# A conditioned mixture-of-experts layer on one core: input buffers, routing pace, split order and due times rearranged

## The chip, the core and the metric

The kernel runs on one core of a Trainium2 chip. The metric is the device time of one execution in microseconds. The engines are named as in the profile: PE is TensorE (PEld its weight loads), DVE is VectorE, ACT is ScalarE, POOL is GpSimd, and SP is SyncE, which here only issues transfers.

## The reference, cut to what matters

8 x 1024 tokens with 512 channels pass through a modulated linear layer, then through a shared gated unit and a routed mixture of 64 experts, 8 of them for each token. The result is added to the input.

```
y  = clip(((x * styles) @ weight.T) * dcoefs + bias, -256, 256)     # styles, dcoefs from cond_512
shared = silu(y @ sh_gate_w) * (y @ sh_up_w) @ sh_down_w            # 512 -> 1024 -> 512
topk_idx, w = route(sigmoid(y @ router_w.T), e_bias)                # 8 groups, best 4, then 8 of 64 experts
for each expert e and its tokens:                                   # 512 -> 256 -> 512
    o = silu(y @ gate_w[e]) * (y @ up_w[e]) @ down_w[e]
    routed[token] += w * o
out = x + shared + routed
```

## The kernel before, in words

All matrix products run in a rounded 32-bit format. Each operand is split into a high part (an ACT copy) and a low part (a DVE subtraction, `split`, L75 its ACT copy, and `sub`, L72), and three products hi·hi, hi·lo, lo·hi are summed in PSUM. So each raw tile that arrives costs one ACT and one DVE instruction before PE can read it.

The work has three stages.

*Conditioning* (to about 240 us). For each of 16 token tiles of 512 tokens (`NT`, `TT`), the modulated layer gives y. It goes to DRAM twice: row by row (`y_d`, for the experts' gathers) and transposed in four slices of 128 channels (`yT_d`, for the shared unit). The last tile, 15, stays in SBUF.

*Shared unit and routing* (240 to 1316 us). `order` is tile 15 first, then 0 to 14; each has `HC` = 8 steps of 128 hidden channels, 128 steps in all, `i` counting them. A step has `gate_up` (24 matmuls, L124), the hidden product in `hidden` (ACT silu, DVE product, split), and `down` of the step before (12 matmuls, L1081). PSUM holds the four sums of a tile in `acc`; at the first step of the next tile `finish` adds the residual rows to them (L1104, DVE) and sends them out (L1105, SP). In the first tile, each step also fetches and splits the shared weights of later steps: `fetch_dn` (L807, tile dnr) and `fetch_gu` (L144, tile gur). In the last steps of each tile `fetch_y` (L1064, tile yr) fetches the four slices of the next tile's y, which `load_y` splits into yh and yl a step later, and `fetch_res` (L1099, tile xn) fetches four blocks of residual rows in the last one. dnr, gur and yr share one tag, "gur", with two buffers; xn has four of its own. All four kinds are issued by SP, in program order; SP waits at an issue until the buffer's last reader is done.

Between these, `route_slots` is a generator that computes on DVE, for eight chunks of 1024 tokens, which slot of which expert each token takes. After each step the loop draws from it as much as a credit allows (`credit`, L1180); each yield gives a cost. What it has ready is scattered by POOL, five per step (`write`, L1051), into a table that the last steps read.

In the last steps the first expert units are begun by hand (`early`, `early_x`): step 126 and step 127 each turn two blocks of gathered rows by PE (L541, into the one pt buffer), split them (xh at L544, xl), and split half of the first unit's gate and up weights (gh at L552, gl).

*Experts* (from 1316 us). 156 units of up to four blocks of 128 slots (20 of one, 16 of two, 120 of four; the last four units, 152 to 155, have 4, 1, 4, 4). A unit gathers its rows (POOL, L537), transposes and splits them, multiplies by gate and up in four parts of 12 matmuls (L564, L573 for the one-block units), takes the hidden product, and for each block does a down of 6 matmuls (L584), weighs it on ACT (oc, L588) and adds it to the output by an indirect transfer of POOL (`scatter`, L591). As two units can hold the same token, the scatters of a unit wait until all those of the unit before it have landed (`chain`). A unit's down needs the whole hidden product's low part; its hidden product's split and its down weights' split wait for the downs of the unit two before it, whose buffers they take. The order of all this is made ahead of time: `plan` gives each task an engine, a length, a lag and a due time; `arrange` simulates the engines and always takes, of the tasks ready on an engine, the one that is due first. The due time of a down is the unit's `ddue` plus the pair from `DOWN`:

```
DOWN = {1: (-8.2, 1.0), 2: (6.6, 5.1), 4: (6.6, 5.1)}
ddue + DOWN[u.nb][0] + DOWN[u.nb][1] * s
```

For a unit of four blocks, `ddue` is 13.76 after the unit's own due time, and the next unit is due 17.76 after it (its 4 x 2.73 of gate and up and 4 x 1.71 of turns and downs).

## Time and profile before

| what | value |
|---|---|
| median of three runs | 3730.5 us (3728.97 to 3731.85) |
| the profiled execution | 3734.11 us |
| its span, first to last instruction | 3732.3 us |
| mean granted TensorE clock | 0.996 |
| first and last matmul | 4.95 us, 3708.1 us |

PE is busy nearly all the span; matmuls overlap in the records, so a busy PE does not by itself say how closely they follow each other, and the distance from start to start is read from the timeline. Engine names with a q (SPq) are issues of transfers, which do not count as busy. The views that the prediction uses are the list of who waited for whom, the timeline of one engine in a window, and the table of windows, whose columns are the stretch and its length, the busy time and instructions of PE, PEld, DVE, ACT and POOL, the granted clock of PE, the DMA engines' busy share and their GB/s.

### The profile page before, as it was taken

Reading aid. Unit: us, or ns where it says so; the run is one execution under the profiler, and the core shown is the slowest. Engines: PE = TensorE matmul, PEld = TensorE weight load, DVE = VectorE, ACT = ScalarE, POOL = GpSimd, SP = SyncE. Lnnn points to the kernel's source line nnn. Section 1 sums busy time; section 2 is a strip of 40 time slices with the busy share of each in tenths; the row PEclk is TensorE's granted clock in tenths of the full one; section 3 lists DMA queues with packets and bytes.
Section 4 is the critical chain, followed back from the end, with each engine's and each line's share of the span. In section 5 each row is a group of like instructions: output and inputs, shape, how many; then the busy total and the mean of one; then the engine's idle time right before and its main releaser. Section 6 shows DMA issues by size and latency. Waiting matters only on the chain. (4 is left out here: it accounts for less than half of the span.)

```text
span 3732.3 us, 49590 instructions
## 1 busy us (share of the span) xinstructions
PE 3686.6 (99%) x17819; PEld 3051.5 (82%) x17819; DVE 2006.0 (54%) x3196; ACT 1736.3 (47%) x2676; POOL 2090.1 (56%) x1597
## 2 busy tenths in 40 slices
PE   8999999999999999999999999999999999999997
PEld 7777888888888888888888888888888888888886
DVE  6766666666552255555455554555555555555553
ACT  6652112111111155555555565555555555555554
POOL 0003676666654055666676666666656656666653
PEclk9999999999999999999999999999999999999998
DMA  8862212222122267777777777777777777777664
GB/s 256 239 173 64 66 35 52 52 47 57 37 50 60 99 166 157 152 150 158 147 141 153 161 183 166 177 177 192 143 174 147 168 145 175 166 157 130 117 118 58
DMA packets 238739, 491.23 MB, mean 132 GB/s; under 512 B 43074, under 2 KB 75858, under 8 KB 230803
## 3 DMA queue, kind: packets, MB, share of 16 engines
q0 software_dynamic: 135840, 280.28, 40.3%
q1 hardware_dynamic: 101651, 206.63, 18.0%
q8 instruction: 142, 2.33, 0.3%
q10 hardware_dynamic: 992, 1.06, 0.1%
q14 instruction: 114, 0.93, 0.1%
HBM read 443.20 MB, written 195.63 MB: 171 GB/s over the span
## 5 line engine op out<-in xcount | busy, mean ns | idle before, releaser
L591 POOL DMA_INDIRECT out<-oc,tokw x532 | 915.6, 1721 | 662.4 <-ACT oc L588 197.8
L564 PE MATMUL pg<-xh,gh 128*128 128x512 f32 (+1 forms) x2176 | 838.7, 385 | 0.0
L1051 POOL DMA_INDIRECT tab_d<-tokw,ad x512 | 566.2, 1106 | 485.3 <-DVE h L136 203.7
L564 PE MATMUL pg<-xh,gl 128*128 128x512 f32 (+1 forms) x2176 | 823.5, 378 | 0.0
L564 PE MATMUL pg<-xl,gh 128*128 128x512 f32 (+1 forms) x2176 | 821.6, 378 | 0.0
L537 POOL DMA_INDIRECT xg<-y_d,tokw x532 | 594.6, 1118 | 357.6 <-PE pt L541 138.5
L72 DVE TENSOR_TENSOR xl<-pt,xh 128x512 fp32r<-128x512 f32 x532 | 352.6, 687 | 413.6 <-ACT xh L544 360.9
L588 ACT ACTIVATE oc<-po,tokw 128x512 f32<-128x512 f32 x532 | 367.6, 691 | 318.0 <-PE po L584 263.2
L564 PEld LDWEIGHTS pg<-xh,gl 128*128 128x128 f32 x2176 | 409.1, 188 | 78.6
L564 PEld LDWEIGHTS pg<-xl,gh 128*128 128x128 f32 x2176 | 409.6, 188 | 71.7
L564 PEld LDWEIGHTS pg<-xh,gh 128*128 128x128 f32 x2176 | 408.8, 188 | 71.1
L584 PE MATMUL po<-dh,hh 128*128 128x512 f32 x1064 | 427.9, 402 | 0.0
L711 DVE TENSOR_TENSOR hf<-hf,pg 128x512 f32<-128x512 f32 x240 | 164.9, 687 | 483.8 <-PE pg L564 458.6
L584 PE MATMUL po<-dh,hl 128*128 128x512 f32 x1064 | 418.1, 393 | 0.0
L584 PE MATMUL po<-dl,hh 128*128 128x512 f32 x1064 | 415.3, 390 | 0.0
L124 PE MATMUL gu<-yh,guh 128*128 128x512 f32 x1024 | 400.9, 391 | 3.4 <-ACT yh L75 3.4
L72 DVE TENSOR_TENSOR gl<-wg,gh 128x1024 fp32r<-128x1024 f32 x312 | 376.2, 1222 | 51.3 <-ACT gh L552 49.3
L124 PE MATMUL gu<-yl,guh 128*128 128x512 f32 x1024 | 401.3, 392 | 0.2 <-DVE yl L72 0.2
L124 PE MATMUL gu<-yh,gul 128*128 128x512 f32 x1024 | 398.8, 389 | 0.0
L544 ACT CAST xh<-pt 128x512 fp32r<-128x512 f32 x532 | 296.9, 587 | 192.4 <-PE pt L541 134.3
L552 ACT CAST gh<-wg 128x1024 fp32r<-128x1024 f32 x312 | 324.1, 1049 | 27.0 <-PE pg L564 23.4
L708 ACT ACTIVATE hf<-pg 128x512 f32<-128x512 f32 x240 | 144.0, 600 | 293.0 <-PE pg L564 279.3
(246 smaller groups left out, 5203.3 us busy)
## 6 DMA issues: line engine op xcount, KB each, us to landing
wg<-in_wexp SPq DMA_DIRECT2D x156, 1024.0 KB
wd<-in_wexp SPq DMA_DIRECT2D x156, 512.0 KB
y_d<-yt SPq DMA_DIRECT2D x64, 256.0 KB
xn<-in_x SPq DMA_DIRECT2D x64, 256.0 KB
out<-xn SPq DMA_DIRECT2D x64, 256.0 KB
xr<-in_xT SPq DMA_DIRECT2D x60, 256.0 KB
yT_d<-yf SPq DMA_DIRECT2D x60, 256.0 KB
yr<-yT_d SPq DMA_DIRECT2D x60, 256.0 KB
```

What stands on the lines that cost most here:

```text
L72: V.tensor_tensor(o, a, b, ALU.subtract)
L124: i_ = PE.matmul(p_, lhsT=w_[:, q * KC + k], rhs=y_[k], start=n == 0, stop=n == 3 * KC - 1)
L537: queued(GP.indirect_dma_start(xg[g % RXG].bitcast(F32), None, y_d, IOA(slot_tok[:, u.block + s:u.block + s + 1], 0)))
L544: S.copy(xh[u.xq][:, :, s * P:(s + 1) * P], pt_of(g).bitcast(F32))
L552: S.copy(a[u.q][:, sl], (wg, wg, wd)[c][u.kind][:, sl])
L564: PE.matmul(out, lhsT=w_[u.q][:, c:c + P], rhs=x_[u.xq][:, k, :w], start=n == 0, stop=n == 3 * KC - 1)
L584: PE.matmul(po[d % 2], lhsT=h_[u.q][:, k, s * P:(s + 1) * P], rhs=w_[u.q][:, k * C:(k + 1) * C], start=n == 0, stop=n == 5)
L588: S.mul(oc[d % ROC], po[d % 2], slot_w[:, u.block + s:u.block + s + 1])
L591: i_ = queued(GP.indirect_dma_start(out, IOA(slot_tok[:, u.block + s:u.block + s + 1], 0), oc[d % ROC], None, compute_op=ALU.add))
L708: si = add((i, "si", m), "ACT", 0.61, 0.15, due + 5.46 * m + 3.1, lambda b=b, f=f: S.activation(hf[f % 3], pg[b % 4], AF.Silu), p, *wait_h ...
L711: mu = add((i, "mu", m), "DVE", 0.69, 0.15, t0, lambda b=b, f=f: V.tensor_tensor(hf[f % 3], hf[f % 3], pg[(b + 1) % 4], ALU.mult), si, p)
L1051: i_ = GP.indirect_dma_start(places, IOA(ad, 0), tw, None)
```

## The change: four edits

1. The slices of the next tile's y (`fetch_y`) are allocated under the tag "xn" with four buffers, together with the residual rows, in place of the tag "gur".
2. The credit of routing is 2.7 for steps 1 to 4, 1.4 for steps 5 to 8 and 2.7 after that; it was 3.4 for steps 1 to 7 and 2.7 after that.
3. In the last two steps, the first two gathered blocks' turn and split come ahead of the weights' split.
4. For the last four units, the due times of the downs are `ddue` + 2.0 + 3.0 s, whatever the number of blocks.

```diff
-                add((i, "down", s), "PE", 1.37, 0.5, ddue + DOWN[u.nb][0] + DOWN[u.nb][1] * s, lambda ...
+            first, step_ = (2.0, 3.0) if len(units) - n <= 4 else DOWN[u.nb]
...
+                add((i, "down", s), "PE", 1.37, 0.5, ddue + first + step_ * s, lambda ...
...
         def fetch_y(j, k):
-            gur["y", j, k] = xb.tile([P, TT], F32, name="yr", tag="gur")
+            gur["y", j, k] = xb.tile([P, TT], F32, name="yr", tag="xn", bufs=4)
...
-                xn[s] = xb.tile([P, C], F32, name="xn", bufs=4)
+                xn[s] = xb.tile([P, C], F32, name="xn", tag="xn", bufs=4)
...
                 if last >= 0:
+                    early_x(2 * last)
                     early(0, "wh", last)
                     early(0, "wl", last)
-                    early_x(2 * last)
...
-                credit = min(credit, 0.0) + (0.0 if not i else 3.4 if i < HC else 2.7)
+                credit = min(credit, 0.0) + (0.0 if not i else 2.7 if i < 5 or i > HC else 1.4)
```

More of the change, by code (lines that the diff above doesn't have):

```diff
@@ L724, in plan @@
                 nd += 1
-                add((i, "down", s), "PE", 1.37, 0.5, ddue + DOWN[u.nb][0] + DOWN[u.nb][1] * s, lambda u=u, s=s, d=d: down_c(u, s, d), *lo, T[i, "wl", 2], get(dns.get(d - 2)))
+                add((i, "down", s), "PE", 1.37, 0.5, ddue + first + step_ * s, lambda u=u, s=s, d=d: down_c(u, s, d), *lo, T[i, "wl", 2], get(dns.get(d - 2)))
                 dns[d] = (i, "oc", s)
```

## The prediction

> **What bounds the kernel now.** I read the page first, then the waits of PE, then the timelines around each wait, last the chain that ended last. The page and the list of PE's waits:

> ```profile
> span 3732.3 us, 49590 instructions
> PE 3686.6 (99%) x17819; PEld 3051.5 (82%) x17819; DVE 2006.0 (54%) x3196; ACT 1736.3 (47%) x2676; POOL 2090.1 (56%) x1597
> ...
> PE py L319 <- DVE xl L303: 6.1, 8, 1.4
> PE ps L260 <- DMA cd<-in_condT: 4.9, 1, 4.9
> PE gu L124 <- ACT yh L75: 3.4, 2, 2.9
> PE py L319 <- ACT xh L302: 3.3, 3, 1.5
> PE pt L541 <- DVE xl L72: 2.4, 2, 1.2
> PE po L1081 <- ACT dnh L75: 0.7, 1, 0.7
> PE po L1081 <- DVE dnl L72: 0.5, 2, 0.2
> ```

> TensorE is busy in 3686.6 of 3732.3 us. Its matmuls of 512 columns start 0.227 us apart (timeline of PE, 322.08 to 322.31), so the span is TensorE's work plus a few holes. No instruction of that work is removed. An edit can pay only in a hole, and the holes sum to 45.7 us: 4.9 before the first matmul, some 16.6 in the waits above, 24.2 after the last matmul (it ends at 3708.1), where this page does not count TensorE at all. The waits of L319 and L260 (14.3 us together) lie in the conditioning stage, which the change does not touch. Left are three places: gu/dnl around 307 to 322 us, pt at 1305 and 1315, and the end.

> **Place 1: the first shared tile, 307 to 322 us.** Timelines of SP, ACT, DVE and PE (start, length, engine, line, operation; in brackets the idle time before it and what ended that):

> ```profile
> 307.55 0.33 SPq L807 DMA_DIRECT2D dnr<-in_shdn  x1
> 308.16 3.74 SPq L1064 DMA_DIRECT2D yr<-yT_d  x2
> ...
> 315.88 0.62 ACT L75 CAST yh<-yr 128x512 fp32r<-128x512 f32 x1 [3.79 <-DMA yr<-yT_d]
> ...
> 316.55 0.80 PE L124 MATMUL gu<-yh,guh 128*128 128x512 f32 x1 [2.94 <-ACT yh L75]
> ...
> 316.50:322.50 6.00, 5.95 (x15) 4.47 (x16) 5.07 (x10) 1.72 (x4) 0.00 (x0) 0.58 0.14 52
> ```

> The fourth slice of the next tile's activations (the second yr issue in the SP row, at 311.57) waited on SP for a buffer of tag gur: the DVE row of dnl ends at 311.54. It lands after 4.3 us (315.88), and L124 sits idle. All four slices share two gur buffers with the raw weights, so each waits for an older split. Behind the idle the granted clock falls: 0.58 of full in the last row's stretch, matmuls 0.427 us apart instead of 0.235. Excess over 0.235 us, start to start: 0.41 at 307.58 (dnl, held up by 5.2 us of routing on DVE from 299.76 to 304.95), then 0.58, 0.49, 0.11, 3.10, 0.49, 0.36 from 312.15 to 317.88, then nine at 0.19. Sum 0.41 + 5.13 + 1.73 = 7.3 us.

> After the change, yr draws on the four xn buffers, empty in this tile. SP does the same eight issues, but the slices stand behind nothing older than gur's turn for their step: slice 0 right behind the issue at 286.82, slice 1 behind the dnr that becomes free at 294.5 (dnl split), slices 2 and 3 behind the one that becomes free at 295.9 (gul split). Issues take 0.33 us, landing 4.3: the last is there by 301.5, while gate_up of the new tile starts at 309.8. Next suspect is DVE: with 2.7 of routing per step for four steps and 1.4 for steps 5 to 8 instead of 3.4, one column pass of 2.5 us (1.13 + 0.69 + 0.69) stands where two stood at 299.76; hl and dnl of that step move up by 2.6 us, and the last yl ends near 307.7. Both causes go. **Gain 7.3 us**; if a slice is still late by one split pair (0.62 + 0.69) and its clock is kept, some 6.

> What this costs: routing counts its steps in the generator's credit. Its first chunk now ends at step 10 instead of 7 (20.6 units of cost at the smaller allowances), so the slot writes begin three steps of 8.2 us later, last one near 1178 + 25 = 1203 us. They go at five per step (8.2 us) and are never read before 1233 us (step 119, holding). 30 us of cover; nothing on TensorE.

> The residual rows now wait on SP for the splits of the same buffers. At the tile turn of 456 us they were issued at 440.88; the last yl there ends at 446.46, so the last row block is issued 4 us later than before and lands near 451. The add that uses it comes at 456.17, behind the last down; the next tile's first down, which needs the PSUM banks, at 462.6. Cover 5 us to the adds and some 9 to TensorE. Cost nothing. In turn, yr waits for the out transfer of the rows (issued to 459.0, landing some 4 us), against a first use two steps before the next turn: over 25 us of cover. Behind a blocked SP stand only transfers of the same kinds, in the same order.

> **Place 2: seam to the experts.** Timeline of DVE and PE:

> ```profile
> 1303.40 1.23 DVE L72 TENSOR_TENSOR gl<-wg,gh 128x1024 fp32r<-128x1024 f32 x1 [0.26 <-ACT gh L552]
> 1304.54 0.68 DVE L72 TENSOR_TENSOR xl<-pt,xh 128x512 fp32r<-128x512 f32 x1
> ...
> 1305.28 0.53 PE L541 MATMUL pt<-idr,xg 128*128 128x128 f32 x4 [1.21 <-DVE xl L72]
> ```

> There is one pt buffer, so the second transpose waits for xl of the first, and xl stands behind gl (1.23) in DVE's order, as xh behind gh (1.05) in ACT's. With the x split ahead, xh can start where gh did (1302.3), xl where hl ends (1303.14, at most 0.1 more), and ends at 1303.85, before the down ends (1304.07 by its issue). Start-to-start excess at the two places: 1.36 and 1.34. **Gain 2.7 us**; lower end 2.2 if semaphores take 0.25 each. The weight split becomes 1.3 us later: it ends near 1314.3 in the last step, and unit 0's first matmul is due at 1316.3 by then. Two us of cover; without it, 1.3 us back.

> **Place 3: the end.** Timeline of POOL (the last scatter-adds; 3704.16 is unit 154's fourth, the four below it unit 155's):

> ```profile
> 3687.32 1.56 POOL L591 DMA_INDIRECT out<-oc,tokw  x1 [7.04 <-ACT oc L588]
> 3692.95 1.56 POOL L591 DMA_INDIRECT out<-oc,tokw  x1 [4.07 <-DMA out<-oc,tokw]
> 3698.44 1.56 POOL L591 DMA_INDIRECT out<-oc,tokw  x1 [3.94 <-ACT oc L588]
> ...
> 3704.16 1.56 POOL L591 DMA_INDIRECT out<-oc,tokw  x1 [0.30 <-issue]
> 3712.12 1.58 POOL L591 DMA_INDIRECT out<-oc,tokw  x1 [6.40 <-ACTq L1193]
> ...
> 3717.75 1.56 POOL L591 DMA_INDIRECT out<-oc,tokw  x1 [0.30 <-issue]
> ```

> A unit's scatters wait until the unit before has landed: 3.9 to 6.4 us after the last instruction's end. The chain of waits ends in the same four rows. By the planner's rule (lowest due of the ready tasks), count from the last unit's due time: its four gate/up parts are due at 0, 2.73, 5.46, 8.19; unit 154's downs at 2.6, 7.7, 12.8, 17.9 before (13.76 + 6.6 + 5.1 s - 17.76), at -2, 1, 4, 7 after. So all four go ahead of the last part; in the trace two of them came behind it (3699.77). Unit 152's downs likewise move up, so its fourth scatter leaves near 3678 instead of 3687.32 and 153's follows near 3684 to 3686. Unit 154's four then leave as their downs allow: about 3694, 3696, 3699.6 and 3701.5.

> The price: two downs (12 x 0.227 = 2.7 us) leave the place where they hid the last unit's silu product and split (3699.77 to 3702.11: 2.34 us). Part 4 now ends at 3702.5, hl at 3704.8, the first down starts at 3704.9: **a new TensorE hole of 2.4 us** right at the end. First oc ends 2.26 later as before (3699.77 to 3702.03), POOL follows 0.27 later: 3707.4; four at a pitch of 1.87 start the last at 3713.0 instead of 3717.75: 4.7 us. The 13.0 us behind it (3719.31 to 3732.3) stay. From this go 0 to 2 us if unit 154's last landing (3703 + 3.9 to 6.4) is late for 3707.4, and 0 to 1.2 for the clock. For the clock: the fall at 314.7 came when TensorE had stood 1.1 us in one piece and 1.75 in the 3.4 us before; pieces of 1.41 and 1.34 at 85.8 and 87.6 left it at full. A hole of 2.4 falls above these more often than not, and would slow six of the first down's matmuls by 0.19 each. **Gain 4.2 us**, range 1.5 to 4.7. It can't turn to a loss: POOL was 8.9 us behind the first oc it could have taken.

> [...]

> **Sum.** 7.3 + 2.7 + 4.2 = 14.2 us. The profiled execution took 3734.1 us (span 3732.3 and 1.8 around it), so it would take 3719.9. The median of the three runs is 3730.5, 3.6 below; taking the gain off it gives **3716.3 us**.

> **Rivals.**
> - *Only the first tile and the seam pay.* If unit 154's last landing still sets the last four scatters (landing after a group of four took 6.4), or the planner's order is not what the chip can follow, the end gives 0 to 1.5: 3719 to 3720.5. For it: that landing was the longest; against: 154's scatters are now spread over 7.5 us. 15%.
> - *The yr wait is the transfer's, not the buffer's.* If landing stays late because the conditioning stage's writes of yT_d are slow, place 1 keeps its 7 us: 3723.3, hardly over the bound of 0.2%. Against: the issue itself stood still until 311.57, and the DMA share is 0.15 at 300 to 307 us. 6%.
> - *Slower: the residual rows starve the tile turn.* Sharing xn puts the row fetch behind the yl splits. It decides once a row block lands more than some 13.5 us after issue (446.5 against 460): from there every us is paid at 14 tile turns. At 2 us over it is 28 us: 3744. For it: SP is in order and one late split blocks all behind it. Against: 4.3 us landing, DMA share 0.3. 4%.
> - *The change doesn't do what it says*: the order of instructions at the seam or in the tail is the same. Each part is in program order or in the due times, so I give it 2%, at 3728.

> The forecast keeps 73%. Its own range is 3715 to 3719; with the first rival and the spread of the three runs (2.9 us) the range is 3713.5 to 3721.5. A measurement here tells about 0.2% (7.5 us) from no change. Faster than that: forecast, first rival, and half of the second, with some of the unnamed lost: 0.89. Within 0.2%: 0.06. Slower: 0.05.

> **What would show it.** L124's wait for yh and L1081's for dnl are gone, the granted clock stays at 1.0 at 300 to 325 us, and the four yr issues stand before 297. PE's wait for xl at L541 is gone. The first POOL issue of the last four comes about 4 us after unit 154's landing, and PE shows a new wait of about 2.4 us for hl ahead of the last four downs. It would be wrong if DVE or SP showed a new wait at the tile turns (L1104 behind in_x), or unit 0's first matmul waited for gl.

## The result, and the profile after

The changed kernel takes 3717.19 us in the median of seven runs (3715.85 to 3720.26), beside 3730.5 (3728.7 to 3732.13) of the kernel before: 13.3 us less, ratio 0.9965 with a 95% interval of 0.9955 to 0.9975. 3716.3 was forecast. On another chip it took 3718.24 beside 3731.68, ratio 0.9963 [0.9950, 0.9977].

The page and PE's waits of the changed kernel (lines of the shared stage stand two further down: L1081 is now L1083, L1064 L1066, L1099 L1101):

```profile
span 3716.6 us, 49611 instructions
PE 3684.8 (99%) x17819; PEld 3053.1 (82%) x17819; DVE 2005.9 (54%) x3196; ACT 1736.5 (47%) x2676; POOL 2086.7 (56%) x1597
...
PE py L319 <- DVE xl L303: 4.3, 4, 1.4
PE py L319 <- ACT xh L302: 2.7, 3, 1.2
PE po L584 <- ACT hh L713: 0.8, 1, 0.8
```

The waits of L124 for yh and yl and of L541 for xl are gone, L1083 keeps only its first one at 256 us, and a new one has come: L584 for hh. The same matmuls run in a span 15.7 us shorter. To see where, I split the span at four marks that both traces have.

| from, to | before | after | change | forecast |
|---|---|---|---|---|
| start, first shared down | 256.80 | 256.13 | -0.7 | 0 |
| to the eighth shared down (tile 15's last) | 65.74 | 58.36 | -7.4 | -7.3 |
| to the first expert matmul | 996.30 | 993.43 | -2.9 | -2.7 |
| to the end of the last scatter | 2400.47 | 2394.87 | -5.6 | -4.2 |
| to the end of the span | 13.02 | 13.79 | +0.8 | 0 |

The first and last rows are scatter between executions: in the nine profiles of kernels with this conditioning stage the first shared down starts between 255.9 and 257.9 us, and in all eleven profiles 12.5 to 14.2 us lie behind the last scatter. The three rows between sum to 15.9; the medians show 13.3, with 9.3 to 16.8 in the interval. The kernel before has one profile, whose execution took 3.6 us more than its median, and that of the changed kernel took 1.2 more than its own. So the distances show where the time went in one execution of each. How much of the 15.9 us other executions gain is not shown; the 1.7 us of slow matmuls in the first tile, for one, stand in that single profile of before.

### The profile page after: what moved, and what is told of

The parts are those of the page before. It is cut to its first block, busy times and chain, and to the rows that moved or that the text cites. A ratio compares the mean times of both kernels' runs of the same rounds, so it can differ in the third digit from the quotient of the medians.

```text
span 3716.6 us, 49611 instructions
## 1 busy us (share of the span) xinstructions
PE 3684.8 (99%) x17819; PEld 3053.1 (82%) x17819; DVE 2005.9 (54%) x3196; ACT 1736.5 (47%) x2676; POOL 2086.7 (56%) x1597
## 4 chain that ended last, share of the span: by engine, by line
PE 98%; DVE 1%; DMA 0%; ACT 0%; issue 0%; POOL 0%; SPq 0%; ACTq 0%; DVEq 0%; POOLq 0%
PE pg L564 38%; PE po L584 20%; PE gu L124 19%; PE po L1083 9%; PE pt L541 4%; PE py L319 4%; PE pg L573 1%; PE plt L344 1%; DMA xr<-in_xT 0%; PE psm L367 0%; ACT yf L325 0%; DVE yl L72 0%; PE pg L578 0%; DVE yt L356 0%; PE ps L1004 0%
## 5 line engine op out<-in xcount | busy, mean ns | idle before, releaser
L591 POOL DMA_INDIRECT out<-oc,tokw x532 | 915.9, 1722 | 663.4 <-ACT oc L588 203.5
L72 DVE TENSOR_TENSOR xl<-pt,xh 128x512 fp32r<-128x512 f32 x532 | 352.6, 687 | 406.6 <-ACT xh L544 405.7
L588 ACT ACTIVATE oc<-po,tokw 128x512 f32<-128x512 f32 x532 | 367.6, 691 | 316.4 <-PE po L584 279.6
L584 PE MATMUL po<-dh,hh 128*128 128x512 f32 x1064 | 428.1, 402 | 0.8 <-ACT hh L713 0.8
L584 PE MATMUL po<-dh,hl 128*128 128x512 f32 x1064 | 418.2, 393 | 0.0
L584 PE MATMUL po<-dl,hh 128*128 128x512 f32 x1064 | 415.3, 390 | 0.0
L72 DVE TENSOR_TENSOR gl<-wg,gh 128x1024 fp32r<-128x1024 f32 x312 | 376.2, 1222 | 52.0 <-ACT gh L552 51.4
L124 PE MATMUL gu<-yl,guh 128*128 128x512 f32 x1024 | 400.2, 391 | 0.0
L124 PE MATMUL gu<-yh,guh 128*128 128x512 f32 x1024 | 399.7, 390 | 0.0
L124 PE MATMUL gu<-yh,gul 128*128 128x512 f32 x1024 | 398.1, 389 | 0.0
L552 ACT CAST gh<-wg 128x1024 fp32r<-128x1024 f32 x312 | 323.9, 1048 | 27.1 <-PE pg L564 27.1
```

The lines of the kernel that those rows point to most:

```text
L72: V.tensor_tensor(o, a, b, ALU.subtract)
L124: i_ = PE.matmul(p_, lhsT=w_[:, q * KC + k], rhs=y_[k], start=n == 0, stop=n == 3 * KC - 1)
L552: S.copy(a[u.q][:, sl], (wg, wg, wd)[c][u.kind][:, sl])
L584: PE.matmul(po[d % 2], lhsT=h_[u.q][:, k, s * P:(s + 1) * P], rhs=w_[u.q][:, k * C:(k + 1) * C], start=n == 0, stop=n == 5)
L588: S.mul(oc[d % ROC], po[d % 2], slot_w[:, u.block + s:u.block + s + 1])
L591: i_ = queued(GP.indirect_dma_start(out, IOA(slot_tok[:, u.block + s:u.block + s + 1], 0), oc[d % ROC], None, compute_op=ALU.add))
```

## The experiments

**One edit taken back at a time.** Four kernels on one chip, each the changed one with one edit as before, called e1 to e4; the four hunks are those of the four kernels in the order of the expectations.

```diff
-            gur["y", j, k] = xb.tile([P, TT], F32, name="yr", tag="xn", bufs=4)
+            gur["y", j, k] = xb.tile([P, TT], F32, name="yr", tag="gur")
...
-                credit = min(credit, 0.0) + (0.0 if not i else 2.7 if i < 5 or i > HC else 1.4)
+                credit = min(credit, 0.0) + (0.0 if not i else 3.4 if i < HC else 2.7)
...
-                    early_x(2 * last)
                     early(0, "wh", last)
                     early(0, "wl", last)
+                    early_x(2 * last)
...
-            first, step_ = (2.0, 3.0) if len(units) - n <= 4 else DOWN[u.nb]
+            first, step_ = DOWN[u.nb]
```

> The changed kernel with the four y slices back in the two gur buffers; routing, split order and due times as changed. Theory (the buffers were the wait): the fourth slice is again issued only behind the split of the last shared down weights. With less routing those splits come some 2.5 us earlier than in the kernel before, so the slice is issued near 308 to 309 us and lands near 313; gate_up of the second tile (L124) waits 2 to 4 us for yh, the clock may fall behind it, and the down that follows starts at 317 to 320 us instead of 314.5. Median 3720 to 3723. Rival (routing on VectorE was the wait): that down stays at 314.5 and the median at 3717.

> The changed kernel with the routing credit of before (3.4 for steps 1 to 7), the y slices in xn. Theory (the buffers): the slices are issued before 297 us all the same; what is left is the 0.4 us wait for dnl near 307 and at most 1 us for a late yl, so the down behind the second tile's first gate_up starts at 315 to 316 us; median 3717 to 3719. Rival (routing was the wait): a wait for yh or yl of 3 us or more is back near 312 to 316 us, median 3721 or more.

> The changed kernel with the weights' split ahead of the gathered rows' split again. Theory: two waits of pt for xl of 1.2 us each are back, and from there PE is 2.7 us later to the end; median 3719.5 to 3720.5. Rival (the seam is hidden by later slack, since the experts' stage has buffers to spare): the two waits are back but the last matmul is not later; median 3717.

> The changed kernel with the due times of before for the last four units. Theory: no wait of PE at the end, the last matmul 1.2 to 1.4 us earlier against the start of the last unit's parts, but the last unit's scatters wait 6.4 us for the landing of the unit before and the last one starts 9.6 us behind the last matmul instead of 2.7; span 4.9 us longer, median 3721.5 to 3722.5. Rival (the end was bound by the matmuls, so the hole eats the gain): span the same within 1 us.

| kernel | first to eighth shared down | to first expert matmul | to end of last scatter | last matmul's end behind the first expert matmul | median us |
|---|---|---|---|---|---|
| before (median on this chip) | 65.74 | 996.30 | 2400.47 | 2389.25 | 3731.0 |
| changed (from the result above) | 58.36 | 993.43 | 2394.87 | 2390.63 | 3717.19 |
| e1: y slices in gur | 59.60 | 993.46 | 2394.86 | 2390.57 | 3720.89 |
| e2: old credit | 58.36 | 993.42 | 2394.83 | 2390.63 | 3718.17 |
| e3: weights first | 58.34 | 996.33 | 2394.97 | 2390.64 | 3720.96 |
| e4: old due times | 58.36 | 993.38 | 2400.54 | 2389.26 | 3721.47 |

(Ratios to before with their intervals, in the order of the last four: 0.9972 [0.9961, 0.9982], 0.9963 [0.9949, 0.9977], 0.9973 [0.9963, 0.9984], 0.9974 [0.9962, 0.9985]. They overlap; the distances do not.)

Each edit shows in its own distance and in no other: routing, with the buffers changed, in none (e2). The split order is worth 2.9 us and the due times 5.7, each in one profiled execution. The medians agree with these sizes only in part: e1, e3 and e4 lie 2.7, 2.8 and 3.3 us above e2, where the distances put 1.2, 2.9 and 5.7 (the median of e3 is 0.5 us above its expected range). So the profiles tell where an edit acts; its size over many executions is sure to a few us only. At the end the two theories of e4 part clearly: with the old due times TensorE finishes 1.4 us sooner, and the last scatter 5.7 us later. The scatters bound the end.

In the first tile the answer is not the one that I had laid down for e1. Either edit by itself does nearly all: the buffers alone give the whole 7.4 (e2), and less routing alone 6.1 (e1). The down behind the second tile's first gate_up starts at 315.53 us, where I had expected 317 to 320. The median of e1 lay in its range all the same; of the 3.7 us above the changed kernel its profile explains 1.2, so that hit was luck. SP and PE of the kernel with the slices in gur:

```profile
302.99 3.75 SPq L1066 DMA_DIRECT2D yr<-yT_d  x2
...
311.47 0.51 PE L124 MATMUL gu<-yh,guh 128*128 128x512 f32 x1 [0.50 <-ACT yh L75]
312.20 0.50 PE L124 MATMUL gu<-yl,guh 128*128 128x512 f32 x1 [0.22 <-DVE yl L72]
```

The fourth slice (second of the x2, 306.41) does wait for a gur buffer again, but it leaves 5.2 us earlier than before (311.57), or 4.3 counted from the first shared down, where I had expected 2.5. In the trace of before, DVE had a routing pass too many at two places of the same chain of buffers: ahead of the dnl behind which the first slice leaves (289.33 to 291.92), and ahead of the hl and the dnl behind which the third leaves (302.37 to 304.96). Counted in the same way, the first slice leaves 1.0 us earlier in e1 and the third 4.3. A third pass too many, ahead of the last dnl (308.05 to 310.63), cost nothing: that dnl waited for its high part on ACT. What is left of the wait, 0.7 us idle, did not bring the clock down (1.00 from 300 to 316 us; from 312.54 on the matmuls start 0.23 us apart), so the 1.7 us of slow matmuls go with it. The wait was thus no single cause: late splits and scarce buffers in series, and it is enough to break one.

**The size of the new hole (e5).** The last unit's downs take the second half of the hidden product first.

```diff
-        for k in range(2):
+        for k in (1, 0) if u.i == 155 else (0, 1):
```

> The changed kernel, but the last unit's downs multiply the second half of the hidden product (k = 1) before the first. Theory (the new hole was 1.4 us and not 2.4 because the three k = 0 matmuls of the first down need only the first half's split, which is done long before): now the first matmul has to wait for the second half's low part or high part, the three matmuls no longer fill the hole, so PE's wait for ACT or DVE grows from 0.8 to 1.5 to 2.2 us, the last matmul ends 0.5 to 0.9 us later against the start of the last unit's first part and the last scatter starts 0.5 to 0.9 us later; the clock may fall if most of the hole lies in one stretch of 3.4 us. Rival (the hole is set by ACT's or PSUM's order, not by which half is needed): the hole stays at 1.4 us.

PE in the changed kernel, and then in this one:

```profile
3691.33 0.39 PE L564 MATMUL pg<-xh,gl 128*128 128x512 f32 x1
3691.56 0.39 PE L584 MATMUL po<-dh,hh 128*128 128x512 f32 x1
3691.78 0.39 PE L584 MATMUL po<-dl,hh 128*128 128x512 f32 x1
3692.01 0.39 PE L584 MATMUL po<-dh,hl 128*128 128x512 f32 x1
3693.22 0.50 PE L584 MATMUL po<-dh,hh 128*128 128x512 f32 x1 [0.82 <-ACT hh L713]
```

```profile
3693.07 0.39 PE L564 MATMUL pg<-xh,gl 128*128 128x512 f32 x1
3694.95 0.50 PE L584 MATMUL po<-dh,hh 128*128 128x512 f32 x1 [1.50 <-ACT hh L713]
```

In the changed kernel three matmuls of the first down run straight behind the last part, since they read the first half, split by 3685.73. With the halves exchanged the idle time grows from 0.82 to 1.50 us, by those three matmuls (3 x 0.227). Excess of the starts over 0.235 us, all of it: 1.34 us against 2.01. The last matmul ends 0.6 us later and the last scatter 0.5 (2395.36 behind the first expert matmul). This kernel has a single run, 3720.29 us, so the reading rests on the distances. The theory holds.

**How long the chain at the end is (e6).** The earlier due times for the last two units alone.

```diff
-            first, step_ = (2.0, 3.0) if len(units) - n <= 4 else DOWN[u.nb]
+            first, step_ = (2.0, 3.0) if len(units) - n <= 2 else DOWN[u.nb]
```

> The changed kernel with the earlier due times for the last two units alone (units 154 and 155). Theory (the end is a chain of scatters through units 152, 153, 154 and 155, each waiting for the landing of the one before, and unit 154's split also waits for unit 152's last down): unit 152's last down stays late, and nearly all of the 5.6 us at the end is lost: last scatter's start 4 to 6.5 us later against the experts' first matmul than in the changed kernel, median about 3721 to 3722. Rival (only the unit next to the last matters): the last scatter as in the changed kernel, median 3717.

POOL's scatters at the end, first of the changed kernel (unit 152's fourth, 153's, the first and fourth of 154's, 155's first), then the same of this one:

```profile
3666.57 2.51 POOL L591 DMA_INDIRECT out<-oc,tokw  x1 [0.30 <-ACT dh L552]
3673.36 1.56 POOL L591 DMA_INDIRECT out<-oc,tokw  x1 [4.28 <-ACT xh L544]
3680.48 1.56 POOL L591 DMA_INDIRECT out<-oc,tokw  x1 [5.55 <-ACT oc L588]
...
3690.00 1.56 POOL L591 DMA_INDIRECT out<-oc,tokw  x1 [2.52 <-ACT oc L588]
3695.60 1.58 POOL L591 DMA_INDIRECT out<-oc,tokw  x1 [4.04 <-ACT oc L588]
```

```profile
3677.54 1.56 POOL L591 DMA_INDIRECT out<-oc,tokw  x1 [7.04 <-ACT oc L588]
3683.06 1.56 POOL L591 DMA_INDIRECT out<-oc,tokw  x1 [3.96 <-DMA out<-oc,tokw]
3688.74 1.56 POOL L591 DMA_INDIRECT out<-oc,tokw  x1 [4.11 <-ACT hf L708]
...
3694.33 1.56 POOL L591 DMA_INDIRECT out<-oc,tokw  x1 [0.30 <-ACT hh L713]
3700.93 1.58 POOL L591 DMA_INDIRECT out<-oc,tokw  x1 [5.04 <-ACT oc L588]
```

With two units, 152's fourth scatter leaves at 3677.54 and holds up the three units behind it, one landing each; 154's four come in one burst, whose landing takes 5.0 us instead of 4.0. The last scatter starts 2397.44 us behind the first expert matmul, against 2393.31 with four units and 2398.97 with none: 1.5 of the 5.7 us are gained. Median 3721.64, ratio 0.9973 [0.9962, 0.9983]. The chain theory holds, at the lower end of its 4 to 6.5 us.

**What is left: the conditioning stage (e7 to e9).** In all these kernels L319 still waits 7 to 9 us for xl and xh near 70, 87 and 133 us. There the table of slots is cleared by five transfers of 832 KB. This version clears in ten of half the size.

```diff
-                if 3 <= j < 8:
+                if 3 <= j < 13:
                     clear(j - 3)
-                if j == 9:
+                if j == 13:
...
-                if j == 11:
+                if j == 14:
                     constants()
...
-    ...f=4)[:, 2 * r:2 * r + 2], ... to_broadcast([E * NR // 40, 2, 8 * P])
+    ...f=4)[:, r:r + 1],         ... to_broadcast([E * NR // 40, 1, 8 * P])
```

> The changed kernel, with the clearing of the slot table in the conditioning stage in ten transfers of half the size over tiles 3 to 12 instead of five over tiles 3 to 7; the two steps on the token numbers that must come behind it move from tiles 9 and 11 to 13 and 14. Theory (the waits of L319 for xl and xh at 69 to 138 us stand behind the clearing transfers in the DMA engines, whose share is 0.86 to 0.90 there): L319's waits, 7.0 us in the changed kernel, fall to 2 to 4 us, one or both falls of the clock (1.7 us each) go, and the first shared down starts 3 to 7 us earlier than 256 us; median 3711 to 3715. Rival (the share is 0.84 to 0.91 at 160 to 220 us too, so the same waits come back later in the stage): the first shared down at 255 to 257 us, median 3717.

> The changed kernel as it stands, beside the one with the spread clearing, on the same chip. Theory (its own first execution was typical): the first shared down at 256 to 258 us, three waits groups of L319 near 70, 87 and 133 us with one to three falls of the clock, the last scatter starting 2393 to 2394 us behind the experts' first matmul; median 3716 to 3719, ratio to before 0.996 to 0.997. Rival (the profiled execution flattered the change): the sum of the three distances is more than 2 us longer than the 15.8 us less than before that its first profile shows.

> The kernel with the spread clearing, once more, beside the changed kernel on the same chip. Theory (the clearing held up the x slices and cost falls of the clock): the first shared down 2.5 to 4.5 us before that of the changed kernel in the same call, one fall of the clock in the conditioning stage instead of two or three, median 2 to 4 us below it. Rival (its first execution was a lucky phase of the clock's windows): first shared down and median within 1.5 us of the changed kernel's.

The kernel with the spread clearing took 3714.68 us the first time (e7), ratio to before 0.9955 [0.9941, 0.9968]. The second time (e9) it took 3715.54 (3712.81 to 3715.92) with the same ratio, beside 3718.24 (3716.85 to 3718.65) of the changed kernel on that chip (e8). The first shared down starts at 253.33 and 253.31 us; the changed kernel's second profile has it at 256.13, like its first. One fall of the clock is left in the stage (at 131.1 or 86.7 us) where the changed kernel has three in its first profile (22.1, 86.9, 134.7) and two in its second (23.5, 132.7). L319's waits, 7.0 and 8.9 us in the changed kernel's two profiles, are 6.0 and 5.8, where I had expected 2 to 4 to be left, and the start of the shared stage moves by 2.8 us, where I had expected 3 to 7. So the clearing as it was is at most a part of the cause. The edit also moves the two steps on the token numbers, which no run separates from it, and waits and falls do not add up to the 2.8 us in either pair; which transfer held up which slice is not shown. Still, the kernel beats both others, by 2.7 us in the medians of the same chip, and no run of the one lies in the range of the other. The second run of the changed kernel repeats the three distances (58.36, 993.41, 2394.87), so its first profile was typical.

## Why the prediction was right, and where a size was off

*Bound and sum.* That an edit could pay only in TensorE's holes or behind its last matmul held: 15.9 us by the profiles' three distances and 13.3 by the medians, 14.2 forecast. The median of 3717.19, 0.9 us from the forecast, is closer than the spread of its own runs and than the terms below, so part of that closeness is luck. The first two rivals, none of the gain at the end or 7 us still lost in the first tile, did not come about. Nor did the tile turns starve: TensorE has no wait there, and at the turn of 448 us the row blocks are issued by 438.2, the adds start at 448.1, so the cover was about what the text said.

*First tile.* The size was right (7.3 forecast, 7.4 between the two profiles), and the clock holds 1.00 from 300 to 325 us where it was 0.86. The slices are issued at 287.48, 293.30, 294.70 and 295.42, before 297 as forecast; SP of the changed kernel:

```profile
287.48 0.43 SPq L1066 DMA_DIRECT2D yr<-yT_d  x1
...
293.30 0.43 SPq L1066 DMA_DIRECT2D yr<-yT_d  x1
...
294.70 1.15 SPq L1066 DMA_DIRECT2D yr<-yT_d  x2
```

Two points were not as told. The two causes are not terms of a sum (e1 and e2). And the slices issued early are not split early, because of a buffer that I had not looked at; ACT of the changed kernel:

```profile
300.68 0.61 ACT L75 CAST dnh<-dnr 128x512 fp32r<-128x512 f32 x1
304.44 1.30 ACT L75 CAST yh<-yr 128x512 fp32r<-128x512 f32 x2 [3.15 <-PE gu L124]
```

ACT waits for PE here: yh has six buffers, the current tile holds four, so the third slice's high part takes one that the current tile's last gate_up still reads. The last yl ends at 306.46, 2.5 us ahead of its tile's first matmul (308.99). It cost nothing, but it is what would be late next.

*Routing's delay.* The last slot write is at 1194.8 us, 16.6 later than before; I had 25 later on an unmoved clock, which is the same less the 8.1 us by which the stage had moved up.

*Seam.* 2.7 forecast, 2.9 measured. xl of the first block now ends at 1295.67 and the second transpose starts at 1295.85, straight behind the down. The 0.25 us for a semaphore, behind the lower end of 2.2, was an assumption of mine that no run shows: before, the second transpose started 0.06 us behind the end of xl (1304.54 + 0.68 to 1305.28). DVE and PE of the changed kernel:

```profile
1294.99 0.68 DVE L72 TENSOR_TENSOR xl<-pt,xh 128x512 fp32r<-128x512 f32 x1
...
1295.85 0.46 PE L541 MATMUL pt<-idr,xg 128*128 128x128 f32 x4
```

*End.* This is the term that was mis-sized: 4.2 forecast, 5.6 measured. The step that failed is "the first down starts at 3704.9: a new TensorE hole of 2.4 us". I let the whole down wait for the whole hidden product, as the planner does. On the chip the down's first three matmuls start at 3691.56, straight behind the last part, and only the fourth waits, up to 3693.22; the hole is 1.3 us, its longest wait is for hh and not for hl (0.82 us), and the first oc is about 1 us sooner than I had it. The 0 to 2 us that I had set aside for unit 154's landing came to 0.2: it landed 4.04 us after its last scatter, when oc had been done for 0.4 (3695.18 to 3695.60; 0.27 was usual). So the last four scatters start at that landing, and not 4 us behind it, as the last paragraph of the prediction says; the 4 us lie between the last scatter's end and its landing. The clock did not fall in the 1.3 us hole (1.00 from 3691.40 to 3698.22 us), nor in the 2.0 us one of e5, behind which the matmuls start 0.23 us apart (3696.02 to 3696.95).

*The clock.* For a fall behind the new hole I had set aside 0 to 1.2 us, an estimate from the fall at 314.7 us. None came: 1.69 of the 3.41 us ahead of that fall were idle, and 0.82 of the 3.41 us that hold the new hole (3691.40 to 3694.81). The last section has the falls of both kernels.

## What to carry to other kernels

Split the span at marks that both traces have and compare distances: effects of 1 to 6 us in 3700 could be put in their places from single profiles this way, where the medians' intervals overlap. Then hold their sizes against the medians, since a profile is one execution. Before adding the gains of two edits in one place, ask whether they cut the same chain; here, in one profile of each, either one gave over 80% of both. And where the last work is a chain of ordered transfers, ask how far back it reaches: here the last two units of four gave a quarter of the gain.

## What the runs showed of the hardware that I had not expected

```profile
82.54:85.95 3.41, 2.00 (x9) 1.30 (x7) 2.26 (x5) 2.55 (x5) 0.00 (x0) 1.00 0.97 293
...
130.35:133.76 3.41, 0.55 (x2) 0.19 (x1) 3.31 (x14) 2.52 (x4) 0.00 (x0) 1.00 0.97 308
311.25:314.66 3.41, 1.72 (x6) 0.53 (x4) 0.99 (x2) 0.62 (x1) 0.00 (x0) 1.00 0.44 99
```

```profile
18.66:22.07 3.41, 3.41 (x34) 3.41 (x32) 2.04 (x3) 2.76 (x4) 0.00 (x0) 1.00 0.90 315
...
83.51:86.92 3.41, 1.47 (x6) 0.63 (x4) 3.00 (x6) 2.86 (x5) 0.00 (x0) 1.00 0.98 326
```

```profile
127.70:131.11 3.41, 1.83 (x7) 0.93 (x7) 3.31 (x13) 2.33 (x4) 0.00 (x0) 1.00 0.91 282
```

After the first, with 1.41 us idle, the clock stayed at 1.00. After each of the other five it was 0.50, for 3.41 or 6.83 us in the two kernels: with 2.86 and 1.69 us idle in the kernel before, none and 1.94 in the changed one, 1.58 in e7. In the fourth stretch, busy throughout, 32 matmuls of eight columns (L277) start 0.11 us apart, so the busy time alone does not sort these falls. An estimate of the work does: counted from the starts, at 0.227 us for every 512 columns, the stretches of the two kernels hold 1.80, 0.23 and 0.99, and 0.13 and 1.02 us of matmul work.

By this count the profiles of the kernel before and of the changed kernel agree from the first full-speed stretch to the last: behind seven stretches, with 0.13 to 1.18 us of work, the clock fell (two of the seven lie at the end of the last matmul), and behind the other 2150, with 1.44 us or more, it stayed. What decides between the two values, and why the clock falls, no run shows.

Two matmul gaps of 1.41 and 1.34 us cost no clock in the kernel before, where two of these stretches meet between them (at 86.0 us; 1.00 from 82.54 to 92.77); two of 1.21 and 1.35 us, with most of both in one stretch, did in the changed kernel (0.50 from 86.92 us). That this makes runs of one kernel differ is not shown: the changed kernel's two profiles have four and two such slow stretches ahead of the first shared down, and both reach it at 256.13 us.
